# Selecting rows of a small table: gathers from HBM, or one load of the table and copies on GpSimd

## The chip, the cores and the metric

The kernel runs on one core of one Trainium2 chip. The metric is the device time of one execution in microseconds (us); three executions are given, and their median is the time of the kernel. Beside them stands one profiled execution, from which all durations in this document come.

## The reference

```python
W = cond_w[cond]                                  # cond: 32 numbers from 0 to 15; W: 32 x 64 x 64
y = einsum('bct,bcd->bdt', x, W)                  # x: 32 x 64 x 1024
y seen as 4 x 512 x 1024                          # 2048 rows of 1024
h = gelu(y @ inter_w + inter_b)                   # inter_w: 1024 x 4096
out = x + (h @ output_w + output_b)               # output_w: 4096 x 1024
```

All is float32. `cond_w` is a table of 16 matrices of 64 x 64, 256 KB in all. For each of the 32 batches one of them is picked by an index that is known only at run time. The first einsum, called "mix" in the kernel, is small. The two large products hold nearly all of the work.

## The kernel before

The two large products are done with Strassen-Winograd at two levels: seven products take the place of eight, at each level, and sums of blocks take the place of the eighth. GpSimd (POOL) forms the sums of the weights, VectorE (DVE) and ScalarE (ACT) those of the other operand and of the results, and TensorE (PE) multiplies. Every matmul of the large products is 128 x 128 by 128 x 256.

The order of the work on each engine is written out by hand. `at(time, fn)` (line 177) enters a step with a number for its time, in units of about one group of eight matmuls; `run()` (line 180) sorts the steps by that number and issues them. The numbers decide only the order in which each engine gets its instructions. What an instruction waits for, a tile that is written or a buffer that comes free, is derived from the tiles. An instruction that waits holds all that stands behind it on its engine. The DMA queues are three: those of SP (`nc.sync`), ACT (`nc.scalar`) and POOL (`nc.gpsimd`).

The start of the kernel, around which the change lies, goes like this:

- `warm` (line 293): eleven matmuls on zeros.
- `start_rows` (line 245): SP loads the 32 indices to all partitions (`cond_sb`), POOL writes row numbers (`row_c`), and DVE forms from both the table rows that each partition needs (`rows`).
- `first_rows` (line 269): for the first two pairs of batches (`NF = 2`) ACT reads the indices into registers and loads four matrices of the table, 16 KB each, with an address from a register.
- `gather` (line 261): for each of the other 14 pairs POOL issues one indirect DMA that fetches 128 rows of 256 bytes (64 rows for each batch of the pair).
- `load_x` (line 289): a pair of batches of x, 512 KB. There are six buffers, so that the seventh load waits for the first mix. `load_w1` (line 439) loads a quarter panel of `inter_w`, 1 MB. The first of these, "11", and two of the x loads are issued on ACT's queue, all others on SP's.
- `mix` (line 313): 32 small matmuls (64 x 128 by 64 x 64) for a pair of batches. `mixed` (line 331) copies the result to SBUF with ACT and DVE. The pairs come in the order 0, 1, 2, 3, 6, 7, 4, 5, 8, 9; the other six follow much later, between large products.
- After the first three mixes, PE does the first two products of the first block, `fA` and `fB` (eight matmuls each, line 544), which need panel "11" of `inter_w` and the first mixes. Then come the other seven mixes, and then the rest of the first block, which begins with `fC`.
- POOL forms the sums of `inter_w` (`inner_w1` line 463, `outer_w1` line 446, all of them through line 186): first those within panel "11", then those within "12", then "s3" and "s1", which need panels "21" and "22".

From `fC` on the steps of both kernels are the same, in the same order. The lines that give the order of the start:

```python
at(-42, first_rows, NF)
at(-43 if j < NF else -41 + 0.1 * j, load_x, i, nc.scalar if i in (2, 3) else nc.sync)
at(-40.75, load_w1, 0, "11", nc.scalar)
at(-39.4 + 0.01 * j, load_w1, 0, n)          # "12", "21", "22"
```

Of the kernel before, what the change touches and what calls it, by code (L numbers as in the profile page):

```python
# [8 lines left out]

F32 = mybir.dt.float32  # L10
I32 = mybir.dt.int32
AF = mybir.ActivationFunctionType
ALU = mybir.AluOpType
PSUM = bass.MemoryType.PSUM
# [61 lines left out]
def kernel(  # L76
# [35 lines left out]
    nc = tc.nc  # L112
    P = 128
    B, C, T = x.shape
    S, _, D = cond_w.shape
    F = inter_w.shape[1]
    assert 2 * C == P and 2 * D == P
    NR = B // 2
# [3 lines left out]
    KQ = NK // 2  # L122
# [20 lines left out]
    x_rows = x.rearrange("(i j) c t -> i (j c) t", j=2)  # L143
    out_rows = out.rearrange("(i j) c t -> i (j c) t", j=2)
    w1_v = inter_w.rearrange("(k p) f -> p k f", p=P)
    w2_v = output_w.rearrange("(s A a u p) n -> a A s u p n", A=2, a=2, u=2, p=P)
    table = cond_w.rearrange("s c d -> (s c) d")


    const = ctx.enter_context(tc.tile_pool(name="const", bufs=1))  # L150
    NL = 6
    b1 = const.tile([P, F // P], F32, name="b1")
    rows = const.tile([P, NR], I32, name="rows")
    wsel_l = const.tile([P, NL, D], F32, name="wsel_l")
    wpool = ctx.enter_context(tc.tile_pool(name="w", bufs=6))
    cpool = ctx.enter_context(tc.tile_pool(name="c", bufs=14))
# [6 lines left out]
    x0 = right1.enter_context(ExitStack())  # L163
    xpool = x0.enter_context(tc.tile_pool(name="x0", bufs=6, side="right"))
    early = x0.enter_context(tc.tile_pool(name="early", bufs=1, side="right"))
    cond_sb = early.tile([P, B], I32, name="cond_sb")
    row_c = early.tile([P, NR], I32, name="row_c")
    wsel_e = early.tile([P, NR - NL, D], F32, name="wsel_e")
    pst = ctx.enter_context(tc.tile_pool(name="pst", bufs=2, space=PSUM))
    acc_pool = ctx.enter_context(tc.tile_pool(name="psacc", bufs=2, space=PSUM))  # L170
# [6 lines left out]
    def at(time, fn, *args):  # L177
        steps.append((time, len(steps), fn, args))
# [63 lines left out]
        return blk(q, b, a)  # L242


    def start_rows():
        nc.sync.dma_start(cond_sb, cond[None, :].to_broadcast([P, B]))
        cond_v = cond_sb.rearrange("p (i j) -> p j i", j=2)
        for j in range(2):
            half = slice(j * C, (j + 1) * C)
            nc.gpsimd.iota(row_c[half, :], [[0, NR]], channel_multiplier=1)  # L250
        for j in range(2):
            half = slice(j * C, (j + 1) * C)
            nc.vector.scalar_tensor_tensor(
                rows[half, :], cond_v[half, j, :], float(C), row_c[half, :],
                op0=ALU.mult, op1=ALU.add,
            )

    def wsel(i):
        return wsel_e[:, i, :] if i < NR - NL else wsel_l[:, i - (NR - NL), :]

    def gather(i):
        nc.gpsimd.indirect_dma_start(
            out=wsel(i),
            out_offset=None,
            in_=table,
            in_offset=bass.IndirectOffsetOnAxis(ap=rows[:, i : i + 1], axis=0),
        )

    def first_rows(n):

        _, idx = nc.values_load_multi_w_load_instructions(
            cond[None, : 2 * n], engines=[mybir.EngineType.Activation],
            min_val=0, max_val=S - 1,
            skip_runtime_bounds_check_because="the reference indexes cond_w by it",
        )
        for i in range(n):
            for j in range(2):
                nc.scalar.dma_start(
                    wsel(i)[j * C : (j + 1) * C, :],
                    cond_w[bass.ds(idx[2 * i + j], 1), :, :].rearrange("s c d -> (s c) d"),  # L280
                )


    XT = {}

    NF = 2
    FIRST = (0, 1, 2, 3, 6, 7, 4, 5)

    def load_x(i, eng=nc.sync):
        XT[i] = xpool.tile([P, T], F32, tag="x0", name=f"x0_{i}")  # L290
        eng.dma_start(XT[i], x_rows[i])

    def warm():

# [141 lines left out]

    W1 = {}

    def load_w1(it, n, eng=nc.sync):
        s = it % NG  # L440
        a, b = int(n[0]) - 1, int(n[1]) - 1
        t = wpool.tile([P, KQ, 4 * P], F32, tag="w", name=f"w{n}_{it}")
        eng.dma_start(t, w1_v[:, ts(b, KQ), ts(2 * s + a, 4 * P)])
        W1[it, n] = t

    def outer_w1(it, n):
# [238 lines left out]


    at(-61, warm)
    at(-60, start_rows)
    order = FIRST + (8, 9)
    at(-42, first_rows, NF)  # L690
    for j, i in enumerate(order[NF:] + tuple(range(NR - NL, NR))):
        at(-50 + 0.1 * j, gather, i)
    for n in Y_ORDER:
        at(-45, new_y, 0, n)
    MIX = 1.06
# [2 lines left out]
    M_AT = {i: t0 + (j - NB) * MIX - (2 if j < NB else 0) for j, i in enumerate(order)}  # L698
    for j, i in enumerate(order):
        t = M_AT[i]  # L700
        if j < 6:
            at(-43 if j < NF else -41 + 0.1 * j, load_x, i, nc.scalar if i in (2, 3) else nc.sync)
        else:
            at(M_AT[order[j - 6]] + MIX + 0.45, load_x, i)
        at(t, mix, i, {3: None}.get(j, "CBC"[j % 2 + (j > 3)]))
        at(t + MIX + 0.3, mixed, i)
    at(M_AT[9] + MIX + 1, store_y1, 8)
    at(-40.75, load_w1, 0, "11", nc.scalar)
    for j, n in enumerate(("12", "21", "22")):
        at(-39.4 + 0.01 * j, load_w1, 0, n)  # L710
    at(-1, lambda: nc.sync.dma_start(b1, inter_b.rearrange("(f p) -> p f", p=P)))
    at(M_AT[9] + MIX + 0.42, end_mix)
    right_sums(M_AT[3] + MIX + 0.5, lambda: inner_y(0, 1))
# [23 lines left out]
    for it in range(nit):  # L737
        a, s = divmod(it, NG)
        b0 = 49 * it
        if it > 0:  # L740
            for n, t in W_LOAD.items():
                at(b0 - 49 + t, load_w1, it, n)
        for n, t in W_AT.items():
            if it == 0:
                t = {1: -10, 2: -8, "s3": -6, "s1": -3}.get(n, t)
            if isinstance(n, str):
                at(b0 + t, outer_w1, it, n)
            else:
                at(b0 + t, inner_w1, it, n)
        for o, p in enumerate(OUTER):  # L750
            b = b0 + 7 * o
            plan_block(
                b, 1, 7 * it + o, (it, p), "f", mm1,
                lambda l, r, it=it, p=p, a=a: (w1_block(it, p, l), y_block(a, p, r)),
            )
            fin = STATE[p][1]
            if fin is not None:
                hidden(b, it, fin)
            if it == NG:
                at(b - 49 + 13, load_y1, Y_ORDER[o])  # L760
                right_sums(b - 49 + 20, lambda p=p: inner_y(1, p), gap=0.8)
        pieces = []
        if it == 1:
            for k in range(KQ):
                e = {}
                t = b0 + 5 + 10.8 * k
                at(t, load_piece, k, e)
                right_sums(t + 5, lambda k=k, e=e: piece_targets(k, e), gap=0.8)
                at(t + 10.5, store_piece, k, e)
        elif it >= 2:  # L770
            n = -(-len(w2_pieces) // (nit - 2))
            for j in range(n):
                i = (it - 2) * n + j
                if i < len(w2_pieces):
                    e = {}
                    t = b0 + 9.5 + 14 * j
                    pc = w2_pieces[i]
                    at(t - 6, load_w2, pc, e)
                    at(t - 2.5, early_t1, pc, e)
                    at(t + 0.6, store_w2, pc, e, ("11", "21", "22"))  # L780
                    right_sums(t, lambda pc=pc, e=e: w2_targets(pc, e), gap=0.8)
                    at(t + 5, store_w2, pc, e, ("t1", "t2", "t3", "t4"))
# [398 lines left out]
```

## Time and profile before

| | |
|---|---|
| three executions | 1349.67, 1355.60, 1355.66 us; median 1355.6 us |
| profiled execution | 1348.21 us, of which the span from the first to the last instruction is 1345.9 us |
| PE busy | 1329.9 us, 99% of the span |
| PE idle between 13.93 and 17.80 us | 3.88 us, its longest wait |
| first `fA` and `fB` | 17.80 to 23.8 us |
| seven further mixes | 23.81 to 37.3 us |
| first `fC` | 38.20 us |

All times in the trace count from the first instruction. PE, DVE, ACT and POOL are the engines; "SPq" and "ACTq" are the instructions that these engines only issue, DMAs above all; q1 is the set of DMA rings fed by SP, q10 that fed by ACT, q0 that fed by POOL. A line of the timeline gives start, length, engine, source line, operation, output<-input, shapes, count, and in square brackets the idle time before it with what ended it.

### The profile page before, as it was taken

How to read it: one execution, taken by the hardware profiler on the slowest of the kernel's cores; microseconds unless marked ns; L12 is line 12 of the kernel's file. 1: busy time of each engine (PE TensorE's matmuls, PEld its weight loads, DVE VectorE, ACT ScalarE, POOL GpSimd, SP SyncE). 2: the span in 40 equal slices, each digit the busy share in tenths (PEclk: the TensorE clock that was granted, in tenths of full speed). 3: DMA queues.
4: the chain of work that ended last, by engine and by line, in shares of the span. 5: the costliest groups of instructions: out<-in, count | busy, mean ns of one | idle time of the engine just before them, and what ended most of it. 6: DMA issues, size and time to landing. Idle time of an engine off the chain costs nothing.

```text
span 1345.9 us, 18976 instructions
## 1 busy us (share of the span) xinstructions
PE 1329.9 (99%) x6542; PEld 1165.1 (87%) x6542; DVE 883.0 (66%) x1581; ACT 487.5 (36%) x985; POOL 959.7 (71%) x599
## 2 busy tenths in 40 slices
PE   8999999999999999999999999999999999999998
PEld 7888888888888888888888888888888888888887
DVE  3766566575787765757648574675766757767776
ACT  2524324243353442524515332333324333333341
POOL 7753756938768396594862967949959689496793
PEclk8999999999999999999999999999999999999999
DMA  8445677787897866758649145183360723916611
GB/s 298 141 159 211 215 213 253 242 274 240 299 354 230 284 214 217 265 196 272 238 177 339 38 162 229 48 306 132 102 274 7 294 99 110 359 40 232 253 47 63
DMA packets 135471, 273.39 MB, mean 203 GB/s; under 512 B 15728, under 2 KB 68208, under 8 KB 123728
## 3 DMA queue, kind: packets, MB, share of 16 engines
q1 hardware_dynamic: 133520, 269.43, 57.8%
q10 hardware_dynamic: 1408, 2.29, 0.5%
q8 instruction: 52, 0.85, 0.3%
q0 software_dynamic: 448, 0.46, 0.1%
q14 instruction: 43, 0.35, 0.1%
HBM read 167.28 MB, written 104.86 MB: 202 GB/s over the span
## 4 chain that ended last, share of the span: by engine, by line
PE 50%; POOL 2%; DVE 2%; DMA 2%; issue 1%; ACT 1%; SPq 0%; DVEq 0%; POOLq 0%; ACTq 0%
PE zA L555 22%; PE zC L555 11%; PE fA L544 6%; PE zB L555 6%; PE fC L544 3%; PE fB L544 1%; DMA out_dram<-xb 1%; POOL h L186 1%; DVE hs L186 1%; PE tp L1035 1%; DMA w2p<-in_L_ffn_output_w_dram 0%; ACT t L206 0%; POOL w2p L186 0%; POOL vt L186 0%; POOL ws L186 0%
## 5 line engine op out<-in xcount | busy, mean ns | idle before, releaser
L544 PE MATMUL fA<-yi,wi 128*128 128x256 f32 x896 | 212.9, 380 | 3.4 <-DVE fX L186 1.5
L186 DVE TENSOR_TENSOR hs<-h,t 128x512 f32<-128x512 f32 x308 | 200.3, 680 | 9.9 <-POOL h L186 5.9
L186 POOL TENSOR_TENSOR h<-h,h 128x1024 f32<-128x1024 f32 x84 | 196.2, 2366 | 2.9 <-DMA out_dram<-xb 2.3
L555 PE MATMUL zA<-hs,wt 128*128 128x256 f32 x840 | 197.9, 379 | 0.3 <-DVE mX L186 0.3
L544 PEld LDWEIGHTS fA<-yi,wi 128*128 128x128 f32 x896 | 169.2, 190 | 29.7 <-issue 2.9
L555 PEld LDWEIGHTS zA<-hs,wt 128*128 128x128 f32 x840 | 158.6, 190 | 21.6 <-issue 0.7
L569 ACT ACTIVATE fD<-fD,b 128x256 f32<-128x256 f32 x128 | 57.9, 500 | 184.4 <-DVE fD L186 179.9
L186 POOL TENSOR_TENSOR wi<-w 128x512 f32<-128x512 f32 x80 | 101.7, 1272 | 30.6 <-PE fC L544 23.2
L186 POOL TENSOR_TENSOR ws<-w,w 128x1024 f32<-128x1024 f32 x32 | 74.9, 2362 | 67.0 <-PE fA L544 47.5
L206 ACT COPY t<-h 128x512 f32<-128x512 f32 x140 | 81.8, 590 | 75.9 <-DVE hs L186 71.3
L206 ACT COPY t<-hs 128x512 f32<-128x512 f32 x112 | 65.4, 588 | 109.3 <-DVE hs L186 109.3
L186 POOL TENSOR_TENSOR wt<-v 128x512 f32<-128x512 f32 x35 | 44.7, 1277 | 81.6 <-DMA v<-w_d 77.7
L186 DVE TENSOR_TENSOR fX<-fA,fX 128x512 f32<-128x512 f32 x104 | 71.4, 686 | 44.5 <-PE fA L544 43.3
L186 POOL TENSOR_TENSOR wi<-w,wi 128x512 f32<-128x512 f32 x40 | 50.8, 1271 | 62.7 <-PE fA L544 56.1
L544 PE MATMUL fC<-y,wi 128*128 128x256 f32 x352 | 83.4, 380 | 0.1
L555 PE MATMUL zC<-hs,v 128*128 128x256 f32 x336 | 79.7, 380 | 0.8 <-DVE hs L186 0.8
L544 PE MATMUL fA<-yi,w 128*128 128x256 f32 x320 | 75.6, 379 | 0.0
L555 PE MATMUL zA<-h,wt 128*128 128x256 f32 x320 | 75.6, 379 | 0.0
L544 PEld LDWEIGHTS fC<-y,wi 128*128 128x128 f32 x352 | 66.8, 190 | 9.5 <-issue 0.5
L555 PEld LDWEIGHTS zC<-hs,v 128*128 128x128 f32 x336 | 63.7, 190 | 9.7 <-DVE hs L186 1.2
L544 PEld LDWEIGHTS fA<-yi,w 128*128 128x128 f32 x320 | 60.9, 190 | 8.2
L555 PEld LDWEIGHTS zA<-h,wt 128*128 128x128 f32 x320 | 60.7, 190 | 8.1
(185 smaller groups left out, 2797.1 us busy)
## 6 DMA issues: line engine op xcount, KB each, us to landing
h<-hs_d SPq DMA_DIRECT2D x56, 1024.0 KB, 5.5
w<-in_L_ffn_inter_w_dram SPq DMA_DIRECT2D x31, 1024.0 KB, 6.2
hs_d<-hs SPq DMA_DIRECT2D x96, 256.0 KB, 3.1
v<-w_d SPq DMA_DIRECT2D x21, 1024.0 KB, 9.2
hs_d<-fD SPq DMA_DIRECT2D x64, 256.0 KB, 3.2
w2p<-in_L_ffn_output_w_dram SPq DMA_DIRECT2D x32, 512.0 KB, 4.9
w_d<-w2p SPq DMA_DIRECT2D x64, 256.0 KB, 2.9
w_d<-w2t SPq DMA_DIRECT2D x48, 256.0 KB, 6.7
```

What stands on the lines that cost most here:

```text
L186: eng.tensor_tensor(o, a, b, ALU.subtract if sub else ALU.add)
L206: nc.scalar.copy(t, src)
L544: nc.tensor.matmul(acc[:, u, :], lt[:, k, ts(u, P)], rt[:, k, :], start=start and u == 0 and k == 0, stop=k == 1, skip_group_check=True,)
L555: nc.tensor.matmul(acc, wl[:, k, :], hr[:, k, :], start=start and k == 0, stop=k == NG - 1, skip_group_check=True,)
L569: nc.scalar.activation(t[:, u, :], t[:, u, :], AF.Gelu_apprx_tanh, bias=b1[:, f : f + 1])
L1035: nc.tensor.transpose(tp[:, v, ts(n0, P)], d[:, n0, ts(v, P)], late["ident"])
```

## The change

The table is loaded as a whole into SBUF, once for the partitions of each half (64 partitions x 16 matrices x 64 numbers, 256 KB each, in pieces of 256 bytes), with two DMAs on ACT's queue. POOL reads the indices into registers, eight at a time, and copies each batch's matrix from the table to its place: 32 copies of 64 x 64 in four groups, two groups at the start, one after the sums of panel "11", one after those of panel "12". The loads of the indices for DVE, the row numbers, the 14 gathers and the four loads with addresses from registers are gone.

All x loads and all panels of `inter_w` are issued on SP. Panel "11" stands after the third x; panels "12", "21" and "22" are moved behind the loads of pairs 4 and 5, which wait for the first and the second mix. The sums of panel "12" and the PSUM banks of some mixes get other numbers.

```diff
-    def start_rows():
-        nc.sync.dma_start(cond_sb, cond[None, :].to_broadcast([P, B]))
...
-    def gather(i):
-        nc.gpsimd.indirect_dma_start(
...
-    def first_rows(n):
+    TAB = []
+
+    def load_table():
+        t = misc.tile([P, S, D], F32, tag="m8", name="tab")
+        for j in range(2):
+            nc.scalar.dma_start(t[j * C : (j + 1) * C], cond_w.rearrange("s c d -> c s d"))
+        TAB.append(t)
+
+    def select(i0, n):
         _, idx = nc.values_load_multi_w_load_instructions(
-            cond[None, : 2 * n], engines=[mybir.EngineType.Activation],
+            cond[None, 2 * i0 : 2 * (i0 + n)], engines=[mybir.EngineType.Pool],
...
+        for k, v in enumerate(idx):
+            i, j = divmod(2 * i0 + k, 2)
+            half = slice(j * C, (j + 1) * C)
+            nc.gpsimd.tensor_copy(
+                wsel(i)[half, :],
+                TAB[0][half, bass.ds(v, 1), :].rearrange("p a d -> p (a d)"),
+            )
...
-    at(-60, start_rows)
     order = FIRST + (8, 9)
-    at(-42, first_rows, NF)
-    for j, i in enumerate(order[NF:] + tuple(range(NR - NL, NR))):
-        at(-50 + 0.1 * j, gather, i)
+    at(-60, load_table)
+    for k, t in enumerate((-59, -58, -9.5, -7)):
+        at(t, select, 4 * k, 4)
...
-        if j < 6:
-            at(-43 if j < NF else -41 + 0.1 * j, load_x, i, nc.scalar if i in (2, 3) else nc.sync)
-        else:
-            at(M_AT[order[j - 6]] + MIX + 0.45, load_x, i)
-        at(t, mix, i, {3: None}.get(j, "CBC"[j % 2 + (j > 3)]))
+        at(-43 + 0.1 * j if j < 6 else M_AT[order[j - 6]] + MIX + 0.45, load_x, i)
+        at(t, mix, i, None if j == 3 else "CB"[j % 2])
...
-    at(-40.75, load_w1, 0, "11", nc.scalar)
+    at(-42.75, load_w1, 0, "11")
     for j, n in enumerate(("12", "21", "22")):
-        at(-39.4 + 0.01 * j, load_w1, 0, n)
+        at(M_AT[order[1]] + MIX + 0.5 + 0.01 * j, load_w1, 0, n)
...
-                t = {1: -10, 2: -8, "s3": -6, "s1": -3}.get(n, t)
+                t = {1: -10, 2: -7.5, "s3": -6, "s1": -3}.get(n, t)
```

More of the change, by code (lines that the diff above doesn't have):

```diff
@@ L10 @@
 F32 = mybir.dt.float32
-I32 = mybir.dt.int32
 AF = mybir.ActivationFunctionType
@@ L146 @@
     w2_v = output_w.rearrange("(s A a u p) n -> a A s u p n", A=2, a=2, u=2, p=P)
-    table = cond_w.rearrange("s c d -> (s c) d")
     const = ctx.enter_context(tc.tile_pool(name="const", bufs=1))
@@ L152 @@
     b1 = const.tile([P, F // P], F32, name="b1")
-    rows = const.tile([P, NR], I32, name="rows")
     wsel_l = const.tile([P, NL, D], F32, name="wsel_l")
@@ L165 @@
     early = x0.enter_context(tc.tile_pool(name="early", bufs=1, side="right"))
-    cond_sb = early.tile([P, B], I32, name="cond_sb")
-    row_c = early.tile([P, NR], I32, name="row_c")
     wsel_e = early.tile([P, NR - NL, D], F32, name="wsel_e")
@@ L242, in lblk @@
         return blk(q, b, a)
-    def start_rows():
-        nc.sync.dma_start(cond_sb, cond[None, :].to_broadcast([P, B]))
[L247 to L256, printed above, removed]
     def wsel(i):
         return wsel_e[:, i, :] if i < NR - NL else wsel_l[:, i - (NR - NL), :]
-    def gather(i):
-        nc.gpsimd.indirect_dma_start(
[L263 to L267, printed above, removed]
-    def first_rows(n):
+    TAB = []
[5 more added lines that the diff above has]
+    def select(i0, n):
         _, idx = nc.values_load_multi_w_load_instructions(
-            cond[None, : 2 * n], engines=[mybir.EngineType.Activation],
+            cond[None, 2 * i0 : 2 * (i0 + n)], engines=[mybir.EngineType.Pool],
             min_val=0, max_val=S - 1,
@@ L275, in first_rows, with load_x @@
         )
[L276 to L281, printed above, removed]
+        for k, v in enumerate(idx):
[5 more added lines that the diff above has]
+            )
     XT = {}
-    NF = 2
     FIRST = (0, 1, 2, 3, 6, 7, 4, 5)
-    def load_x(i, eng=nc.sync):
+    def load_x(i):
         XT[i] = xpool.tile([P, T], F32, tag="x0", name=f"x0_{i}")
-        eng.dma_start(XT[i], x_rows[i])
+        nc.sync.dma_start(XT[i], x_rows[i])
     def warm():
@@ L437, with load_w1 @@
     W1 = {}
-    def load_w1(it, n, eng=nc.sync):
+    def load_w1(it, n):
         s = it % NG
@@ L442, in load_w1 @@
         t = wpool.tile([P, KQ, 4 * P], F32, tag="w", name=f"w{n}_{it}")
-        eng.dma_start(t, w1_v[:, ts(b, KQ), ts(2 * s + a, 4 * P)])
+        nc.sync.dma_start(t, w1_v[:, ts(b, KQ), ts(2 * s + a, 4 * P)])
         W1[it, n] = t
```

## The prediction

> **What bounds the kernel now.** I read the page first, then PE's timeline of the first 60 us.
>
> ```profile
> span 1345.9 us, 18976 instructions
> ...
> PE 1329.9 (99%) x6542; PEld 1165.1 (87%) x6542; DVE 883.0 (66%) x1581; ACT 487.5 (36%) x985; POOL 959.7 (71%) x599
> ```
>
> PE is never without work for long, and the change alters nothing in what PE does or in which order. So only time at which PE stands still, or runs slowly, can be won or lost. PE's timeline shows where that is at the start:
>
> ```profile
> 1.33 7.09 PE L300 MATMUL warm<-zeros 128*128 128x256 f32 x22 [1.33 <-DVE zeros L297]
> 8.35 5.58 PE L322 MATMUL py<-wsel_e,x 64*128 64x64 f32 x96
> 17.80 3.75 PE L544 MATMUL fA<-y,w 128*128 128x256 f32 x8 [3.88 <-DMA w<-in_L_ffn_inter_w_dram]
> 21.35 2.53 PE L544 MATMUL fB<-y,w 128*128 128x256 f32 x8
> 23.81 13.51 PE L322 MATMUL py<-wsel_e,x 64*128 64x64 f32 x224
> 38.20 1.97 PE L544 MATMUL fC<-yi,wi 128*128 128x256 f32 x8 [0.88 <-DVE ys L347]
> ```
>
> The first mix starts at 8.35, as the zeros end (1.33 + 7.09 = 8.42): the first matrices of the table cost PE nothing. Then PE waits 3.88 us for panel "11", and after it does sixteen matmuls in 6.0 us (17.80 to 23.81) which later take 1.73 us for eight (starts 45.18, 46.91, 48.63). The table of stretches says why:
>
> ```profile
> 8.35:13.93 5.58, 5.57 (x97) 5.43 (x96) 1.51 (x4) 2.45 (x5) 4.06 (x6) 1.00 0.99 376
> 13.93:17.80 3.87, 0.00 (x0) 0.03 (x1) 0.76 (x2) 0.65 (x2) 2.96 (x4) 0.74 1.04 378
> 17.80:23.80 6.00, 6.00 (x16) 4.56 (x16) 0.00 (x0) 0.59 (x1) 4.94 (x6) 0.60 1.05 369
> ```
>
> The third column from the right is the granted clock: it falls in the wait, and fA and fB run at 0.60. The second from the right, the DMA share, is 1.0: the 16 DMA engines are full from 8 us on, so the order in which loads are served sets what PE waits for. The wait with its slow clock costs 3.9 + (6.0 - 3.45) = 6.4 us; this is what a better order could win. From 38.20 on everything follows PE, and a start later or earlier by some us moves the end by as much.
>
> **What the change removes.** The gathers take 14 x (0.94 + 0.30) = 17.4 us of POOL, from 5.0 to 22.4, before the sums of panel "11" (22.42 to 27.6). These are first used by fC at 38.20; 10 us cover them, so freeing POOL wins nothing by itself. The gathers carry 14 x 32 KB, the new table 512 KB: DMA bytes stay. The two DVE instructions (0.17 us each) and ACT's four loads with registers are not on PE's path.
>
> **What it adds: the mix now waits for the whole table.** The first mix needs POOL's first two copies, and these need both table loads, 2 x 1024 pieces of 256 bytes, 128 for each of the 16 DMA engines, on ACT's rings (q10). Meanwhile SP's rings (q1) hold x 0, 1, 2, panel "11", x 3, 6 and 7; only the load behind them waits, for the first mix. How do two full queues share? The queue view from 13 to 14 us, and one from 6.6 to 7.0, in which ACT's 256-byte loads go (columns: packets, MB, share of the 16 engines):
>
> ```profile
> q1 hardware_dynamic: 60, 0.24, 61.2%
> q10 hardware_dynamic: 60, 0.12, 31.3%
> ```
>
> ```profile
> q10 hardware_dynamic: 172, 0.04, 42.8%
> ```
>
> In the first, q1 has packets of 4 KB (x) and q10 of 2 KB (the panel): as many of one as of the other, though half the bytes. One packet costs an engine 0.612 x 16 us / 60 = 163 ns, or 83 ns. In the second, 172 packets cost 0.428 x 16 x 0.4 us / 172 = 16 ns. So packet goes against packet, and the table has small ones: its 128 per engine meet all of SP's, 48 of 4 KB and 32 of 2 KB. The table is last home, though it was issued first.
>
> Here a rule of the Trainium skill speaks: DMA: Bandwidth & Descriptors, "Queues, rings and completion order" and "SWDGE vs HWDGE vs iDMA". An engine takes turns between queues by packets, and a packet is typically some 9 to 17 descriptors, preferably up to 4096 bytes. By that, 16 pieces of the table would go in one turn; 128 pieces need 8 turns, and the table is home early. But in the row every 256-byte piece is a packet of its own; in this trace only the gathers' rows come together (16 packets of 2 KB for 128 rows). I take the row and keep the rule as a rival.
>
> The sum for the first mix. Fast flow begins at 3.9 us now (the first bytes at 1.9, but they are the indices sent to 128 partitions, which goes); between 1.9 and 3.9 I take 3.0. SP's packets: 48 x 0.163 + 32 x 0.083 = 10.5. The table: 128 x 0.016 = 2.0 (at the gathers' row, 0.01 us for 256 bytes, 1.3; at twice the row 4.1). That is 15.5 for a mean engine. The slowest is later: counted in the same way, panel "11" before (8 x, 32 of its own, 16 of x and 9 of panel "12" between them, 4 gather packets: 7.7 us from 8.0) is home at 15.7, and PE got it at 17.8. So 2.0 more: 17.5. Two copies on POOL: no row is alike; between its memset (0.10, 128x1) and the sum of 128x512 at 1.27 / 512 = 2.5 ns a number, 64 numbers make 0.16 + 0.1; two of them and PE's start 0.6. **The first mix starts at 18.1** instead of 8.35, with ends of 16 and 20. POOL's reading of indices (ACT's took until 4.0) lies under this.
>
> **From there to fC.** Three mixes 5.6, the copies before fA 0.7 (13.95 + 0.65 against 13.93), fA and fB: panel "11" has been home for long, so the 3.9 us wait is gone. But PE now idles from 8.4 to 18.1, longer than the 3.9 us that took the clock away before, so the slow stretch only moves into the mixes. By the row it costs 2.55. The skill (TensorE: Matmul & The Clock Gate, "Part 1: The HAM clock gate") says that the clock is halved after an idle window of about 3.4 us and comes back after a fully busy one, the windows running free: 3.4 to 6.8 us at half clock, a loss of 1.7 to 3.4. The row lies in the middle; I take it, and the rule's ends for the range. fB ends at 18.1 + 5.6 + 0.7 + 6.0 = 30.4 instead of 23.8: **6.6 us later** (5.7 to 7.5 by the rule).
>
> The moved loads must then be hidden. x 4 and 5, panels "12", "21", "22" and x 8 stand on SP behind the first mix (3.6 us at half clock, so 18.1 + 3.6). First bytes 1.2 later; 24 x 0.163 + 96 x 0.083 = 11.9; the slowest engine 2.0: x 8 is home 18.7 us after the first mix began. Mix 8 is due after fB and five mixes of 1.93, at 12.3 + 9.7 = 22.0. Cover 3.3 us. x 9, issued after mix 3, comes 1.3 later and is due 1.9 later. On POOL, counted from the first mix: 16 copies 4.2, second reading of indices 3.2, sums of "11" 5.2, eight copies with their reading 5.3, sums of "12" 5.2 (their panel is home at about 12), again 5.3, then "s3", "s1" and "s2" at 4.7 each: 42.5. The first use of "s2" is 22.1 us after fC, so at 12.3 + 14.4 + 22.1 = 48.8. Cover 6 us; without it each us is PE's. The buffer of the table comes free for a later x load at about 28; that pair's mix is due at 44. So fC, and with it the end, comes 6.6 us later: 1348.2 + 6.6 = 1354.8 in terms of the profiled execution (2.3 us of it around the span). The median of the runs is 7.4 above that execution; **1355.6 + 6.6 = 1362.2 us.**
>
> **Rivals.** *The table is home early* (not slower). If the table's pieces go in turns of 4 KB, or get ahead while SP still issues its first loads, 8 to 16 packets of x stand between: 3.0 + 2.0 + 1.3 to 2.6, and some slack, is 7 to 9. The mix starts at about 9.3, the clock stays, panel "11" is home at about 13, fB ends at 9.3 + 5.6 + 0.7 + 3.5 = 19.1: 4.7 us earlier, 1351. For it: the table is issued first on its queue, at once. Against it: the equal counts. It decides when the mix starts before 11.3 with a clock lost, or 13.8 with the clock kept; from there on the change is slower. *In between*: several small pieces for each large one; the mix at 11 to 16, -1 to +4 us, no difference to be told. *Still later*: the flow begins at 3.9, pieces cost 32 ns, x 8 comes behind its mix: mix at 21 or more, +9 to +13, 1365 to 1369. For it: the indices' 128-byte packets went only slowly (1.9 to 4.0 for eight per engine).
>
> **How the numbers follow.** Table last, +5 to +9: 0.62 (own range 1360 to 1365). Early: 0.13. In between: 0.14. Still later: 0.11. A measurement of this kernel tells about 0.5%, 6.8 us, from no change; 6.6 lies at that border. Slower by more: 0.62 x 0.6 + 0.11, and some of the border by the spread of runs, 0.50. Faster by more needs the early table and a favourable median (the runs spread by 6 us): 0.12. Within: 0.38. The range takes in the early table and half of the late one: 1350 to 1367.
>
> **What would show it.** PE's first mix at 16 to 20 behind POOL's copies, POOL's first copy waiting for the table; q10 with 256-byte packets until q1's have run out; clock 0.5 in the mixes; fA without a wait for the panel; fC at 43 to 47. A first mix at 9 to 11 refutes the main step; a first mix as forecast with fC beyond 48 refutes the cover of x 8 or of POOL.

## The result and the profile after

The changed kernel takes 1355.7 us (median of 22 executions, 1352.5 to 1357.7). The kernel before, run in turn with it, takes 1349.1 us (22 executions, 1347.7 to 1357.1). The ratio is 1.003, with a 95% interval of [1.0016, 1.0043]: slower, by less than the 0.5% that the prediction set as its bound. That ratio is near to that of the means (1355.5 to 1351.5 us); the two medians lie further apart, 6.5 us or 0.48%, because most of the 22 executions of the kernel before are in the lower of the two groups that follow. A second comparison on another chip gave 1354.4 against 1350.9 us, ratio 1.0019 [1.0004, 1.0033].

One thing has to be known to read these numbers: the executions of the kernel before spread over two groups, a lower one, most of it at 1347.5 to 1350 us with a mean granted clock of 0.997, and an upper one, most of it at 1353 to 1358 us with 0.991 or 0.992; a few lie between them. Of the three times given at the start (1349.67, 1355.60, 1355.66) two are of the upper group, of the 22 nine. The changed kernel has one group only, 1352.1 to 1357.7 us with clocks of 0.992 to 0.995 in both comparisons.

The profiled execution of the changed kernel took 1353.98 us. Its page:

```profile
span 1352.0 us, 19009 instructions
...
PE 1334.0 (99%) x6542; PEld 1168.5 (86%) x6542; DVE 882.3 (65%) x1579; ACT 487.6 (36%) x985; POOL 953.3 (71%) x615
```

PE is busy 4.1 us longer for the same 6542 matmuls (1329.9 before), and the span is 6.1 us longer. The timeline of PE at the start shows where (the profile counts each matmul of the source twice, and so do the numbers here):

```profile
1.33 6.62 PE L282 MATMUL warm<-zeros 128*128 128x256 f32 x22 [1.33 <-DVE zeros L279]
8.44 0.43 PE L304 MATMUL py<-wsel_e,x 64*128 64x64 f32 x2 [0.48 <-POOL wsel_e L261]
14.82 10.50 PE L304 MATMUL py<-wsel_e,x 64*128 64x64 f32 x94 [5.96 <-POOL wsel_e L261]
25.25 3.58 PE L526 MATMUL fA<-y,w 128*128 128x256 f32 x8
28.67 1.89 PE L526 MATMUL fB<-y,w 128*128 128x256 f32 x8
30.50 13.58 PE L304 MATMUL py<-wsel_e,x 64*128 64x64 f32 x224
44.00 1.99 PE L526 MATMUL fC<-yi,wi 128*128 128x256 f32 x8
```

Two matmuls of the first mix run at 8.44, with the half of the table that has landed. Then PE waits 5.96 us for POOL's second copy. The wait for panel "11" ahead of fA is gone. The three mixes, which took 5.58 us before, take 10.50; fC begins at 44.00 instead of 38.20, 5.8 us later. The table of stretches gives the reason (after the length come the busy times of PE, PEld, DVE, ACT and POOL; the third number from the right is the granted clock, then come the DMA share and GB/s):

```profile
8.44:14.82 6.38, 0.43 (x2) 0.29 (x2) 0.00 (x0) 0.00 (x0) 0.23 (x1) 0.74 1.05 381
14.82:25.25 10.43, 10.43 (x94) 10.31 (x94) 1.67 (x4) 1.79 (x5) 8.25 (x18) 0.50 0.53 164
25.25:30.50 5.25, 5.25 (x18) 4.10 (x17) 0.83 (x2) 1.03 (x3) 1.67 (x8) 0.69 1.04 397
30.50:44.00 13.50, 13.50 (x225) 13.23 (x224) 10.65 (x23) 8.16 (x21) 10.72 (x15) 1.00 0.59 154
```

The clock falls to a half in the wait, at 11.44, and stays there through the rest of the first three mixes, although PE has work in every one of those 10.43 us. It is back at 28.51, as fA ends. The 0.88 us that PE waited ahead of fC before are gone, which is why fC is only 5.8 us later and the mixes ahead of it 6.7 (30.50 against 23.81).

What the wait waits for is in POOL's timeline, whose copies end it:

```profile
8.15 0.23 POOL L261 COPY wsel_e<-tab 64x64 f32 x1 [7.70 <-DMA tab<-in_L_cond_weights_dram]
14.54 1.97 POOL L261 COPY wsel_e<-tab 64x64 f32 x7 [6.15 <-DMA tab<-in_L_cond_weights_dram]
17.43 2.19 POOL L261 COPY wsel_e<-tab 64x64 f32 x8 [0.92 <-issue]
...
28.48 1.10 POOL L261 COPY wsel_e<-tab 64x64 f32 x4 [3.60 <-issue]
```

The first half of the table is home at 8.15, the second at 14.54. The queue view says in what company (packets, MB, share of the 16 engines), from the start to 8.1 us and then from the start to 14.5 us:

```profile
q1 hardware_dynamic: 342, 1.27, 58.5%
q10 hardware_dynamic: 1619, 0.41, 27.3%
```

```profile
q1 hardware_dynamic: 1195, 3.52, 74.5%
q10 hardware_dynamic: 2080, 0.52, 19.1%
```

A few of these packets are of 4 bytes, 16 at the end of each load (32 of q10's 2080). Without them, 1602 pieces of the table had been served by 8.1 us against 310 of SP's packets of 4 KB, some five for one. The other 446 took until 14.5, while 805 large ones of 2 or 4 KB went by. Five for one is a mean and not a rule: from 5 to 6 us both queues had 71 packets, from 6 to 7 q10 had 607 and q1 had 41, and from 8.1 to 10 they were level again (203 to 213).

### The profile page after: what moved, and what is told of

The parts are those of the page before. It is cut to its first block, busy times and chain, and to the rows that moved or that the text cites. A ratio compares the mean times of both kernels' runs of the same rounds, so it can differ in the third digit from the quotient of the medians.

```text
span 1352.0 us, 19009 instructions
## 1 busy us (share of the span) xinstructions
PE 1334.0 (99%) x6542; PEld 1168.5 (86%) x6542; DVE 882.3 (65%) x1579; ACT 487.6 (36%) x985; POOL 953.3 (71%) x615
## 4 chain that ended last, share of the span: by engine, by line
PE 87%; DVE 5%; POOL 3%; issue 2%; ACT 2%; DMA 0%; POOLq 0%; DVEq 0%; ACTq 0%
PE fA L526 26%; PE zA L537 23%; PE fC L526 12%; PE zC L537 11%; PE fB L526 6%; PE zB L537 6%; PE py L304 3%; DVE hs L181 1%; POOL h L181 1%; PE tp L1013 1%; ACT t L201 1%; DVE fX L181 1%; POOL w2p L181 1%; DVE mZ L181 0%; DVE fV L181 0%
```

## The experiments

The first four ran on one chip, where the kernel before gave 1357.8 us (median of 19, 1356.9 to 1359.3, with clocks of 0.992 to 0.994; none is of its lower group, so ratios under 1 come easily there). The next four ran on a second chip, where it gave 1350.7 (median of 48, 1347.4 to 1361.1). Of the last three, two ran on a third chip and one on a fourth. A ratio is always to the kernel before on the same chip.

### The table ahead of x

```diff
-            nc.scalar.dma_start(t[j * C : (j + 1) * C], cond_w.rearrange("s c d -> c s d"))
+            nc.sync.dma_start(t[j * C : (j + 1) * C], cond_w.rearrange("s c d -> c s d"))
```

The two loads are now the first on SP, so nothing shares the engines with them.

> The changed kernel, with the two loads of the table issued on SP's queue ahead of the first x instead of on ACT's queue. My theory: the second half of the table lands at 14.5 us only because it shares the DMA engines with SP's loads; ahead of them in one queue its 128 pieces per engine need some 2 to 3 us. It then lands by 6, the zeros (to 8) hide it, the first mix runs at about 8.5 with the full clock, panel 11 is home by about 13, fB ends at 18.5 to 20 instead of 30.5, and fC starts at 32 to 34 instead of 44.0: 10 to 12 us less than the changed kernel, 4 to 6 us less than the kernel before. Rival (256-byte pieces are slow by themselves, or POOL is): the first mix stays at 12 or later and the time is that of the changed kernel to within 3 us.

Measured: 1347.4 us (1345.7 to 1347.9, 5 executions), ratio 0.9922 [0.991, 0.9935]. Each load of the table lands some 3.7 us after its issue (10.2 in the changed kernel). PE's timeline:

```profile
8.96 5.58 PE L304 MATMUL py<-wsel_e,x 64*128 64x64 f32 x96
14.46 1.99 PE L526 MATMUL fA<-y,w 128*128 128x256 f32 x8
...
29.97 6.65 PE L304 MATMUL py<-wsel_e,x 64*128 64x64 f32 x64 [2.52 <-DMA x<-in_x_dram]
36.55 3.78 PE L526 MATMUL fC<-yi,wi 128*128 128x256 f32 x8
```

It was the sharing with SP's loads that held up the table: without it the first mix is where the zeros end, the clock stays through the first mixes, and fA starts 10.8 us earlier than in the changed kernel. Part of this is lost again. PE now comes to pair 8 before its x is there, waits 2.52 us, and the clock falls once more: 64 mix matmuls take 6.65 us (3.7 at full clock) and fC 3.78. The cover of pair 8's load, which the prediction had at 3.3 us, goes as soon as PE is early.

### A longer stretch of zeros

```diff
-        for _ in range(11):
+        for _ in range(26):
```

PE multiplies zeros until about 14.3 us, so it does not stand idle before the table.

> The changed kernel with 26 instead of 11 matmuls on zeros, so that PE is at work until the table's second half lands at 14.5. My theory: of the 5.8 us by which fC comes later, 4.9 are the slow clock, for the 94 matmuls of the first three mixes take 10.5 us after the wait and 5.6 at full clock. With PE kept busy the clock stays, the three mixes take 5.6 us, fB ends at about 25 and fC starts at about 38.5 to 39.5: 4.5 to 5.5 us less than the changed kernel, level with the kernel before. Rival (the mixes are slow for another reason, the loads or the copies): the mixes still take about 10 us and fC stays at 43 to 45.

Measured: 1347.3 us (1346.1 to 1354.2, 6 executions), ratio 0.9931 [0.9914, 0.9948]. Four of the six show a clock of 0.999 or 1.0 and 1346.1 to 1348.2 us; the other two, the profiled one among them, 0.996 and 1351.5 and 1354.2. The timeline of PE in that one, and its table of stretches:

```profile
15.41 8.04 PE L304 MATMUL py<-wsel_e,x 64*128 64x64 f32 x94 [0.68 <-POOL wsel_e L261]
```

```profile
14.73:18.14 3.41, 2.73 (x48) 2.73 (x50) 0.50 (x2) 0.65 (x2) 1.62 (x7) 1.00 0.49 192
18.14:21.55 3.41, 3.41 (x37) 3.41 (x36) 1.09 (x3) 0.74 (x2) 2.88 (x9) 0.50 0.63 175
```

Where the clock holds, this kernel is at 1346 to 1348 with the table as late as ever; the changed kernel, on other chips, took 1354 to 1356 by its medians. So most of what the changed kernel loses is the clock. By time and clock four executions went as the theory has it (none of them has a trace). The profiled one did not: after a wait of only 0.68 us the clock went from 1.00 to 0.50 at 18.14, in the middle of the mixes, while PE was busy without a gap.

The stretches above are cut where they are for a reason. By the clock records of all of these traces the clock changes only in steps of 3.41 us: here it is full for four steps up to 18.14 and half for three after it, and the stretches at half clock around the mixes are 3.41, 6.83, 10.24, 13.65, 17.07, 20.48 and 30.72 us long. The wait of 0.68 us lay whole in the step from 14.73 to 18.14, in which PE was busy for 2.73 of 3.41 us, with small matmuls alone, and the clock was lost at its end. A step filled by small matmuls kept it (the seven mixes of the changed kernel).

### The order alone, and the table alone

The order alone: the kernel before with its gathers, and the loads in the order of the changed kernel.

```diff
-            at(-43 if j < NF else -41 + 0.1 * j, load_x, i, nc.scalar if i in (2, 3) else nc.sync)
+            at(-43 + 0.1 * j, load_x, i)
...
-    at(-40.75, load_w1, 0, "11", nc.scalar)
+    at(-42.75, load_w1, 0, "11")
...
-        at(-39.4 + 0.01 * j, load_w1, 0, n)
+        at(M_AT[order[1]] + MIX + 0.5 + 0.01 * j, load_w1, 0, n)
```

The number for the sums of panel "12" moves with the order.

> The kernel before, gathers and all, with only the order of loads from the change: all x loads and panel 11 on SP, panel 11 after the third x, the other panels behind the loads of pairs 4 and 5. My theory: the first mix stays at about 8.4, panel 11 is home before the third mix ends at 14, the wait of 3.9 us and the slow clock at fA go, fB ends at 18 to 20 and fC starts at 32 to 34: 4 to 6 us less than the kernel before. Rival (the new order is itself what costs, since the loads behind the first mix come late): fC at 38 or later, no gain.

Measured: 1359.1 us (1357.7 to 1360.5, 13 executions), ratio 1.0008 [1.0, 1.0016]. The gain expected of the order did not come: fC begins at 49.09. The timeline of PE and its table of stretches:

```profile
11.20 4.78 PE L322 MATMUL py<-wsel_e,x 64*128 64x64 f32 x49 [1.07 <-DMA wsel_e<-in_L_cond_weights_dram]
...
29.57 3.48 PE L544 MATMUL fA<-y,w 128*128 128x256 f32 x8
```

```profile
16.60:26.00 9.40, 3.67 (x17) 2.40 (x16) 0.93 (x3) 1.24 (x4) 7.95 (x8) 0.50 0.09 23
```

First ACT's loads of single matrices come late, beside the filled queue of SP. Then, from 16.6 to 26.0, PE is busy for 3.67 us only, in small pieces between gaps that the profile ends by nothing ("issue"), and the DMA engines rest too (share 0.09). POOL's gathers go on until 22.5. What held PE, ACT and DVE there was not found; this stays open.

The table alone: the changed kernel with the loads of x and of the panels on the queues and in the order of the kernel before.

```diff
-        at(-43 + 0.1 * j if j < 6 else M_AT[order[j - 6]] + MIX + 0.45, load_x, i)
+        if j < 6:
+            at(-43 if j < 2 else -41 + 0.1 * j, load_x, i, nc.scalar if i in (2, 3) else nc.sync)
+        else:
+            at(M_AT[order[j - 6]] + MIX + 0.45, load_x, i)
...
-    at(-42.75, load_w1, 0, "11")
+    at(-40.75, load_w1, 0, "11", nc.scalar)
...
-        at(M_AT[order[1]] + MIX + 0.5 + 0.01 * j, load_w1, 0, n)
+        at(-39.4 + 0.01 * j, load_w1, 0, n)
```

The number for the sums of panel "12" goes back too.

> The changed kernel with the load order of the kernel before: x 2, panel 11 and x 3 on ACT's queue, now behind the table, and panels 12, 21, 22 early on SP. My theory: the table lands late for the same reason (12 to 16 us), and panel 11 later still, since it stands behind the table and shares with x 6, x 7 and panels 12 and 21: home at 18 to 22. The first mix starts at 12 to 16, the mixes run on the slow clock, fB ends at 28 to 33 and fC starts at 42 to 47: 4 to 9 us more than the kernel before. Rival (order of loads decides, the table costs nothing): within 2 us of the kernel before.

Measured: 1349.6 us (1348.1 to 1350.2, 5 executions), ratio 0.9937 [0.9924, 0.995], on the chip where the kernel before was never in its lower group; fC is 2.3 us later than in the profile of before that the prediction used. Neither expectation came: it is not slower than before there, and fC, at 40.49, is ahead of the 42 to 47 forecast. PE's timeline:

```profile
11.60 10.49 PE L304 MATMUL py<-wsel_e,x 64*128 64x64 f32 x94 [2.69 <-POOL wsel_e L261]
...
40.49 1.99 PE L526 MATMUL fC<-yi,wi 128*128 128x256 f32 x8
```

With panel "11" and two of the x loads behind the table on ACT's queue, less stands beside the table on SP, and the first mix is 3.2 us earlier than in the changed kernel (a little earlier, too, than the expectation had it). The clock is lost all the same, at a wait of 2.69 us, and the mixes take the same 10.5 us. So of the 5.8 us by which fC is later in the changed kernel, 2.3 come with the table and 3.5 with the new order of the loads (44.00 - 40.49), by one profile of each kernel.

### The kernel before once more

The source is unchanged; what was wanted is a profile of its upper group.

> The kernel before, unchanged, with a new profile. Its executions fall into two groups, 1348 and 1355 to 1358 us, at granted clocks of 0.997 and 0.992 to 0.994; the profile that the forecast was made from lies in the lower. My theory, from the order-only kernel: in the upper group PE, ACT and DVE get their instructions late between 10 and 25 us while POOL issues its gathers (idle times that end with issue), so that the mixes lie open to 25 us and the clock stays low for 15 us and more; fC starts at 45 to 49 instead of 38.2. Rival: the first group of matrices or panel 11 lands late from HBM, and PE waits for a DMA in one piece; no idle times that end with issue. If this profile falls into the lower group, it looks like the first.

Measured: 1353.5 us (1347.7 to 1358.8, 20 executions, ratio 1.0008 [0.9991, 1.0025]): nine at 1347.7 to 1351.4 with clock 0.996 or 0.997, eleven at 1353.2 to 1358.8 with 0.990 to 0.992. The profiled one is of the upper group, 1354.99 us with a span of 1352.7. PE's timeline, and the table of stretches:

```profile
16.75 3.25 PE L544 MATMUL fA<-y,w 128*128 128x256 f32 x8 [2.10 <-DMA w<-in_L_ffn_inter_w_dram]
...
29.36 12.53 PE L322 MATMUL py<-wsel_e,x 64*128 64x64 f32 x128 [1.73 <-DVE y L347]
42.83 3.75 PE L544 MATMUL fC<-yi,wi 128*128 128x256 f32 x8 [0.94 <-DVE ys L347]
```

```profile
31.04:41.88 10.84, 10.84 (x102) 10.66 (x100) 5.25 (x11) 4.04 (x11) 10.84 (x6) 0.50 0.26 15
```

This is the 7 us between the two groups, as far as one profile of the upper one can show it (spans of 1352.7 and 1345.9). In the profile that the prediction used, the seven mixes ran in one piece and at full clock. Here PE waits 1.73 us after the third of them, the clock falls, and four mixes take 12.53 us instead of 7.7 (128 x 60 ns); fC is cold too, and begins at 42.83 instead of 38.20. No "issue" gaps of the kind of the order-alone run are in it. The view names a copy of DVE for the 1.73 us, but in the earlier profile the same copy began at 30.34, after PE had begun the fourth of the mixes. The x of that mix, pair 4, fits better. It stands on SP behind panels "12", "21" and "22", and in the earlier profile it was issued at 12.91 and landed 16.3 us later, at 29.25:

```profile
x<-in_x_dram SPq DMA_DIRECT2D x1, 512.0 KB, 16.3
```

There PE began that mix at 29.39, with nothing to spare. In the profile here PE was ready for it at 27.63, as panel "11" landed 1.1 us earlier (16.61 against 17.67) and fA and fB took 5.3 us and not 6.0; it began it at 29.36. This trace lacks the landing of pair 4's x, but has that of pair 5's, which stands behind it, at 30.49 (30.52 in the other). So the upper group's extra wait comes, as far as these traces tell, of PE being early for a load that keeps its time. What moves panel "11" from execution to execution was not followed up.

### Without the gathers

```diff
-        nc.gpsimd.indirect_dma_start(
-            out=wsel(i),
-            out_offset=None,
-            in_=table,
-            in_offset=bass.IndirectOffsetOnAxis(ap=rows[:, i : i + 1], axis=0),
-        )
+        nc.gpsimd.memset(wsel(i), 0.0)
```

The kernel before, with zeros in the place of 14 pairs' matrices.

> The kernel before, with each of the 14 gathers on POOL replaced by a memset of its target; the 14 matrices are left out, the four that ACT loads stay. Theory (the gathers are what holds the other engines' instructions back in the upper group): no idle times that end with issue in the mixes, all executions in the lower group, 1344 to 1349, whatever the kernel before does on this chip; 14 gathers carry only 0.46 MB of some 8 MB, about 1.2 us of transfer. Rival (they have nothing to do with the groups): the executions follow the kernel before within 3 us.

Measured: 1347.8 us (1345.4 to 1351.7, 22 executions), ratio 0.9978 [0.9964, 0.9991]; fC at 38.02 in the profile, with 4.1 us of wait for panel "11". POOL's 17 us are worth nothing on PE's path in that profile (38.02 against 38.20), as the prediction had it. But only one execution of 22 has a clock under 0.996, and none is above 1352; of the kernel before on this chip 25 of 68 have 0.992 or less. So the gathers have a part in the wait that makes the upper group, and the trace shows which: without their transfers the x of pair 4, issued at 10.79, lands 17.0 us later, at 27.8 and not at 29.25, while PE comes to its mix at 29.05. Now it has 1.2 us to spare.

### The table first and x of pairs 8 and 9 early

To the first experiment is added:

```diff
-    for j, n in enumerate(("12", "21", "22")):
-        at(M_AT[order[1]] + MIX + 0.5 + 0.01 * j, load_w1, 0, n)
+    for t, n in ((M_AT[order[1]] + MIX + 0.5, "12"), (-6.5, "21"), (-3.5, "22")):
+        at(t, load_w1, 0, n)
...
-                t = {1: -10, 2: -7.5, "s3": -6, "s1": -3}.get(n, t)
+                t = {1: -10, 2: -7.5, "s3": -3.2, "s1": -3}.get(n, t)
```

> The table-first kernel, where mix 8 waited 2.5 us for its x at 27.45, lost the clock by it and reached fC at 36.55 with fC itself at half clock. Here x 8 is issued ahead of panel 21 and x 9 ahead of panel 22, and nothing else moves. Theory: x 8 is home by 25, the wait of 2.5 us, the slow last two mixes (6.6 instead of 3.8 us) and the slow fC (3.6 instead of 1.8) go: fC at 31 to 33, 6 to 7 us less than the table-first kernel, 1340 to 1342. Rival (the loads of panels 21 and 22, now later, hold up POOL's sums and PE behind them): PE waits for POOL behind fC, and the gain is under 3 us.

Measured: 1341.6 us (1340.3 to 1348.7, 11 executions), ratio 0.9933 [0.991, 0.9956]; six executions with clock 0.999 or 1.0 at 1340.3 to 1341.6, five with 0.996 or 0.997 at 1345.0 to 1348.7. The profile is one of the five. PE's timeline, then POOL's:

```profile
27.95 7.38 PE L304 MATMUL py<-wsel_e,x 64*128 64x64 f32 x64 [1.76 <-POOL wsel_e L261]
```

```profile
15.19 2.20 POOL L261 COPY wsel_e<-tab 64x64 f32 x8 [7.86 <-issue]
...
27.66 1.10 POOL L261 COPY wsel_e<-tab 64x64 f32 x4 [5.01 <-issue]
```

The wait for x is gone, and another has come in its place: POOL's copy for pair 8. Ahead of its second and third group of copies POOL stands for 7.86 and 5.01 us, which the timeline puts down to "issue". This is where it reads eight indices into registers. A reading is two loads, by their names one of the tensor's address (`_ptr`) and one of the values. The view of their source line shows those of the second group (duration in ns, then the start in us):

```profile
L253 POOLq TENSOR_LOAD <-in_itok_B_dram_ptr x1: 4816/4816/4816, 6.1 to 6.1; - x1
...
L253 POOLq TENSOR_LOAD <-in_itok_B_dram x1: 3984/3984/3984, 11.0 to 11.0; - x1
```

That is 8.8 us, with the DMA engines full. The fourth reading, from 32.6 on with the DMA engines at rest, took 0.88 and 0.95 us.

### Large matmuls between the mixes

The changed kernel, with 32 matmuls on zeros of the large shape (16 in the source) after the first mix; the zeros get a tile of their own for it.

```diff
+    def probe():
+        t = acc_pool.tile([P, 2, W], F32, tag="A", name="probe")
+        for _ in range(16):
+            nc.tensor.matmul(
+                t[:, 1, :], XT["z"][:, :P], XT["z"][:, P:], start=True, stop=True
+            )
...
+    at(-10, probe)
```

> The changed kernel with 16 matmuls of the large shape on zeros between the first mix and the second. Theory: the small matmuls of the mixes (64 x 128 by 64 x 64) keep PE busy to 10.4 of 10.4 us and do not bring the clock back, while matmuls of 128 x 128 by 128 x 256 do; so the clock goes back to 1.0 within 3.4 to 6.8 us of the start of the zeros, and mixes 1 and 2 take 3.6 us together instead of 7. Rival (the clock comes back after a set time, however PE is used): it stays at 0.5 until about 29 us, as in the changed kernel.

One execution, 1358.1 us, with more work than the changed kernel; it is here for its timeline and stretches:

```profile
15.49 3.67 PE L312 MATMUL py<-wsel_e,x 64*128 64x64 f32 x30 [5.96 <-POOL wsel_e L261]
19.09 9.65 PE L288 MATMUL probe<-zeros 128*128 128x256 f32 x32
28.67 3.79 PE L312 MATMUL py<-wsel_e,x 64*128 64x64 f32 x64
```

```profile
15.49:19.09 3.60, 3.60 (x30) 3.48 (x30) 0.00 (x0) 0.30 (x1) 2.30 (x10) 0.50 0.29 114
19.09:24.00 4.91, 4.91 (x13) 3.92 (x13) 0.83 (x2) 0.44 (x2) 4.45 (x8) 0.50 0.34 107
...
24.98:28.67 3.69, 3.69 (x19) 2.98 (x17) 0.00 (x0) 0.00 (x0) 2.31 (x9) 1.00 0.02 7
```

After the same wait of 5.96 us, the clock is back 5 us after the large matmuls begin (at 24.14), and the two mixes behind them run at 59 ns a matmul (3.79 / 64). In the changed kernel the small matmuls kept PE as busy for 10.4 us and the clock stayed at a half, 112 ns each. Here the large ones work on zeros; in the other traces, where they are fA, fB or fC, every return of the clock also comes within large matmuls, 2.7 to 5.5 us after the first of them, and none within mixes. It is the kind of work that brings the clock back, not being busy. Which part of it counts, the rows, the columns or the length of a matmul, was not tried.

### The indices of ten pairs read before the first sums

To the kernel with table and x early:

```diff
-    for k, t in enumerate((-59, -58, -9.5, -7)):
-        at(t, select, 4 * k, 4)
+    for t, i, n in ((-59, 0, 5), (-58, 5, 5), (-7, 10, 6)):
+        at(t, select, i, n)
```

> The table ahead of x on SP and x of pairs 8 and 9 ahead of panels 21 and 22, as before, and now the indices of the first ten pairs are all read before POOL's first sums (five pairs and five), those of the six late pairs after the sums of panel 12. In the kernel without this step the seventh mix onward waited 1.76 us for POOL's copy of pair 8, whose reading of indices took 5.0 us, and the clock was lost from 28.98 to 39.22. Theory (the reading of indices was that wait): no wait of PE after the first mix, mixes 7.7 to 13.2 and 16.9 to 29.9, fC at about 31, clock 1.0 in all of them, 1340 to 1342 us in nearly all executions, that is 0.990 of before at its better executions. Rival (POOL is late by its sums, not by the reading): POOL now reads five pairs first, its sums of 11 start later than 17.5, PE waits for wi in the first block after fC, fC at 31 but 1344 or more. Second rival (x of pair 8 is late as well, the copy hid it): a wait for x at about 26.5, clock lost again, 1345 to 1348.

Measured: 1361.2 us (1357.7 to 1362.9, 9 executions), ratio 1.0063 [1.0041, 1.0086]. All three expectations missed. POOL's timeline, then PE's:

```profile
28.57 2.81 POOL L261 COPY wsel_e<-tab 64x64 f32 x10 [20.66 <-issue]
```

```profile
29.40 21.03 PE L304 MATMUL py<-wsel_e,x 64*128 64x64 f32 x192 [8.92 <-POOL wsel_e L261]
```

The reading of ten indices, begun at 6.5 us with the DMA engines full, took 5.1 and 16.6 us for its two loads, and POOL stood for 20.7. PE waited 8.92 us, and six mixes ran cold:

```profile
29.40:50.36 20.96, 20.96 (x192) 20.84 (x192) 9.15 (x19) 7.25 (x18) 19.17 (x30) 0.50 0.04 3
```

Here small matmuls kept PE busy for 21 us, with the DMA engines at rest, and the clock stayed at a half all the while. The order of the copies was not the trouble. The reading is, and it has no fixed price: the last one, of twelve indices with the DMA engines at rest, took 0.96 and 1.37 us.

### The changed kernel once more

> The changed kernel as it is, for more executions of both kernels in turn on one chip. Theory (the changed kernel always loses its clock in the first mixes and has one group; the kernel before has two, at 1348 with clock 0.997 and at 1353 to 1359 with 0.991): after at 1353 to 1357 with clock 0.992 to 0.994 in nearly all, and the ratio by medians depends on how many executions of before fall in its upper group: 1.005 where a quarter does, 1.000 where all do. Rival (before's two groups belong to the run and both kernels share them): after has executions near 1348 too, in the same rounds as before.

Measured: 1354.4 us (1352.1 to 1357.4, 22 executions) against 1350.9 (1347.5 to 1358.1, 30), ratio 1.0019 [1.0004, 1.0033]. The changed kernel has clocks of 0.992 to 0.995 and nothing near 1348. Of before, 18 executions lie at 1347.5 to 1352.0 with 0.994 to 0.997, and 12 at 1353.9 to 1358.1 with 0.991 or 0.992. The two groups are the kernel's before, not the chip's: the same turns gave the changed kernel no low one. How often the kernel before falls in each differs from chip to chip, though (9 of 22, 25 of 68 and 12 of 30 in the upper one, and on the first chip of the experiments none in the lower).

### Indices from SBUF

To the kernel with table and x early, in the order that it had:

```diff
+        nc.sync.dma_start(cond_sb, cond[None, :])
         for j in range(2):
             nc.sync.dma_start(t[j * C : (j + 1) * C], cond_w.rearrange("s c d -> c s d"))
...
         _, idx = nc.values_load_multi_w_load_instructions(
-            cond[None, 2 * i0 : 2 * (i0 + n)], engines=[mybir.EngineType.Pool],
+            cond_sb[0:1, 2 * i0 : 2 * (i0 + n)], engines=[mybir.EngineType.Pool],
```

> As the kernel with the table ahead of x and x of pairs 8 and 9 ahead of panels 21 and 22, with one change: the 32 indices (128 bytes) are first loaded to SBUF, by the first DMA on SP, and POOL reads its registers from there and not from HBM. In that kernel POOL's second and third reading of eight indices took 7.86 and 5.01 us while the DMA engines were full, and PE waited 1.76 us for the copy of pair 8; with ten indices at once the second reading took 20.7 us and PE waited 8.9. Theory (the reading goes to HBM behind the transfers and that is its time): from SBUF each reading takes under 1.5 us, no wait of PE after the first mix, fC at 31 to 32, clock 1.0 throughout, 1340 to 1342 us in nearly all executions, ratio 0.990 to 0.994. Rival (the time is POOL's own, for moving values to registers or for fetching instructions): gaps of 5 to 9 us stay, PE waits for the copy of pair 8, 1345 to 1349 in half of the executions as in the kernel without this step. The first copy may come up to 2 us later, behind the load of the indices (a DMA's landing), which the zeros hide up to 8.4.

Measured: 1340.7 us (1340.0 to 1341.5, 6 executions, clock 0.999 or 1.0 in each) against 1350.1 (1347.9 to 1358.4, 11), ratio 0.9924 [0.99, 0.9949]. PE's timeline, then POOL's:

```profile
8.47 5.58 PE L306 MATMUL py<-wsel_e,x 64*128 64x64 f32 x96
13.98 1.99 PE L528 MATMUL fA<-y,w 128*128 128x256 f32 x8
...
17.63 13.57 PE L306 MATMUL py<-wsel_e,x 64*128 64x64 f32 x224
31.13 1.99 PE L528 MATMUL fC<-yi,wi 128*128 128x256 f32 x8
```

```profile
5.92 4.25 POOL L263 COPY wsel_e<-tab 64x64 f32 x15 [0.90 <-DMA tab<-in_L_cond_weights_dram]
13.24 1.27 POOL L182 TENSOR_TENSOR wi<-w 128x512 f32<-128x512 f32 x1 [3.07 <-DMA w<-in_L_ffn_inter_w_dram]
```

POOL goes from its eighth copy to its ninth without a gap. A reading from SBUF is a single load, and the four of them took 0.57 to 0.78 us, three of them while the DMA engines were full (ns, first and last start in us):

```profile
L255 POOLq TENSOR_LOAD <-cond_sb x4: 565/569/781, 2.0 to 25.9; - x4
```

PE does not wait from the first mix to fC, the clock is full from there on, and fC begins at 31.13, 7.1 us earlier than in the kernel before. This version beats both kernels in every execution that was taken.

## Why the prediction was wrong

**The base.** The step that failed is the last one of the sum: "The median of the runs is 7.4 above that execution", and 1355.6 + 6.6. In terms of the profiled execution the forecast was 1354.8, and the profiled execution of the changed kernel took 1353.98. Only by adding the same 6.6 us to 1355.6 did it become 1362.2, with a chance of 0.50 for more than 0.5%. The 7.4 us were taken for something that lies on both kernels. They are a loss of clock that the kernel before alone has in its seven mixes, in some of its executions, as the profile of its upper group shows (four mixes in 12.53 us). The changed kernel doesn't have this second loss in its profiles: its seven mixes run in one piece, 13.58 us at clock 1.00 (and 13.57 in the second profile). Its own order of loads takes the cause away, for the x of pair 4 now goes ahead of panels "12", "21" and "22": it landed at 22.38 and its mix began at 35.90. So the changed kernel always pays once, in its first three mixes, what the kernel before pays at times in its last four. By the means it is 6.9 us slower than the lower group of before and level with the upper one (1355.5 against 1348.6 and 1355.7; 5.3 slower and 1.6 faster in the second comparison), and the measured 0.2 to 0.3% is a mean over before's two groups. Three times of 1349.67, 1355.60 and 1355.66 beside a profile of 1348.21 at clock 0.997 were a sign that there were two groups, and the question to put was which of them the changed kernel would be in.

**The table.** "The first mix starts at 18.1" was 3.3 us too late (14.82). The mechanism was there: the last of the table came home when 1115 of the 1280 large packets that were listed on SP's queue at the start (80 for each engine) had gone by. The equal counts, though, held only at times (5 to 6 us, 8.1 to 10); up to 8.1 us some five small packets went for one large, and at times fifteen (607 to 41). So the rival's turns of several pieces have their part in the first half, home at 8.15, and PE's two matmuls at 8.44. As the second half is waited for too, this didn't help. For the mean engine the sum said 15.5, and the landing was at 14.5; the 2.0 us added for the slowest engine were not there. With the table not sharing at all, it is home at 4 to 6 us, which settles that it was the sharing.

**The clock.** "The slow stretch only moves into the mixes", at 2.55 us, was too small. The mixes lost 5.0 us (94 matmuls at 112 ns instead of 58) and fA 1.6 (3.58 against 1.99): 6.6 us, against the 1.7 to 3.4 that the prediction estimated from the rule in the Trainium skill's TensorE: Matmul & The Clock Gate ("Part 1: The HAM clock gate"). The row came from a wait with large matmuls behind it, and the rule counts busy time and asks for no shape. The length of its windows, some 3.4 us, is that of the steps in these traces; that a fully busy window brings the clock back is not so here. Small matmuls followed, and they filled three whole steps (14.85 to 25.10) at half clock; the step after them, of large ones, ended it. The run with large matmuls between the mixes shows that these make the difference. The loss of 4.1 us more than forecast, less 0.7 us for a gap before fA that did not occur, cancels the 3.3 us of the table: fB was to end at 30.4, and the next mixes began at 30.50. That the profile met the forecast of fC (5.8 us later, against 6.6) is thus mostly luck.

**The covers.** They held in the changed kernel: PE does not stand between 14.82 and the end of fC, though POOL stood for 0.92, 3.60 and 2.17 us over its readings of indices. The x of pair 8 landed at 35.25 and its mix began at 39.57, a cover of 4.3 us where the sum had 3.3. They held because PE was late. In the versions where it is not, pair 8's x (2.52 us) and POOL's reading of indices (1.76 us) come out. The prediction's cover of 6 us for POOL looked at "s2" alone, and not at the copy of pair 8, and the 3.2 us for a reading were taken from ACT's at the start, when the DMA engines had little to do.

**The rivals.** The early table is the one that the runs made real: fB ends at 18.2 in the first experiment (16.29 + 1.89), where the rival said 19.1. "In between" (the mix at 11 to 16, no difference to be told) is nearest to what the changed kernel did by its place, 14.82, and by its result. It had 0.14; its mechanism was half there, and its price, -1 to +4 us, met the 4.0 us between the means but not the 5.8 us at fC.

## What to carry to other kernels

Before a change is added to a median, look whether the executions of the kernel before form one group; if not, find what its groups differ by, and ask which of them the changed kernel will be in. A wait ahead of small matmuls costs more than itself: let PE multiply something large through it, or have large products right behind it, since small ones run at half speed until large ones come. A small load that everything waits for belongs ahead of the large ones, on the same queue; and register values that are read while the DMA engines are full are best read from SBUF.

## What was not expected of the hardware

- Small matmuls (64 x 128 by 64 x 64) hold a full clock for 13.57 us without a gap, but neither 10.4 nor 21 us of them brought a lost one back; 32 large matmuls on zeros did so in 5 us.
- The clock changed only in steps of 3.41 us. A wait of 0.68 us between the zeros and the mixes was once followed by half clock, at the end of the step in which it lay, 2.7 us after the mixes had begun again; four of six executions of that kernel kept it. How much of a step may be idle was not found.
- POOL's reading of eight indices from HBM into registers is two loads, of 0.9 us each with the DMA engines at rest. Beside full ones they took up to 5.1 us each (16.6 for the values of ten indices), though not always: in the run with the table alone the second and third reading took 2.0 and 2.1 us in all. From SBUF it is one load of 0.57 us, beside full DMA engines too.
- Two queues shared the engines at some five packets of 256 bytes for one of 4 KB up to 8.1 us, and in single microseconds at anything from one for one to fifteen for one.
- In the run with the order alone PE, ACT, DVE and the DMA engines nearly stood for 9 us without a cause in the profile. It was not followed up.
